# Edge stage of a graph layer: new pacing of its groups, and all output products of the attention ahead of the score table

## The chip, the core and the metric

The kernel runs on one core of a Trainium2 chip, in one launch. The metric is the device time in microseconds (us). Before the change three runs gave 2243.9 (median), 2245.11 and 2240.32.

Five engines have queues of their own and are ordered among each other by semaphores only: PE (TensorE, matrix products), DVE (VectorE), ACT (ScalarE), POOL (GpSimd, which here issues the gathers and scatters) and SP (SyncE, which here issues the loads of weights). All the code around the change is scheduled by hand: each engine executes its instructions in the order in which the program writes them.

## The reference

A graph of 625 nodes of 1024 features and 10000 edges goes through two layers. Layer 0 adds three things to the node matrix `x`, and layer 1 (which the change touches only in its first pieces) five more:

```
xn = layernorm(x)
# graph attention (GATv2): xl, xr = two projections of rms-normed, down-projected xn
e[edge]  = sum over 64 features of att * leaky(xl[src] + xr[dst])      # 4 heads
alpha    = softmax of e over the edges that end in the same node
graph    = segment_sum(alpha * xl[src]) @ W_up
# linear attention: q, k = elu(..)+1, v; 16 heads
mix      = ((q @ (k^T v)) / (q . sum k)) @ W_o + b_o
x        = x + graph + mix
x        = x + ternary_ffn(layernorm(x))          # weights rounded to -1, 0, 1
# layer 1: SAGE graph layers, linear attention again, attention and experts
```

The kernel turns the softmax into dense products: exp(e) of each edge is scattered into a table of 625 x 625 x 4 numbers in HBM, the table is read back tile by tile and multiplied with a matrix CT of edge counts.

## The kernel before

Nodes lie in five tiles of 125 (`t` = 0 to 4), features in eight blocks of 128 (`k`).

**The stream.** `do(prep, pe, after, after2)` writes a piece for PE; its `after` (work for DVE and ACT on the result) is written at the next call of `do`, its `after2` at the one after. So one piece of PE always stands between a product and its evaluation.

**The edge stage** (from about 48 us) lays two things over each other. On PE run the pieces of the linear attention: `key(t)` and `value(t)` for two halves of the features, each with up to six `count()` products (which build CT) behind it, then `states`, `query(m)`/`answer(m)` for m = 0 to 7, then `mixed(t)`, the output product of tile t with W_o (16 matmuls of 512 columns for each of two halves). Under them run 40 groups of edges: 39 of two chunks of 128 edges and one of 16 edges, 79 chunks in all. A chunk needs two gathers (`ga`, `gb`: rows of xl and xr, line L588) and one scatter (into `table`, L602) on POOL; a group needs three passes of DVE (L596, L568, L569) and a short limit (L571), and an exp on ACT (L575). `ga` and `gb` have four buffers each.

A **beat** writes a step of that second row: in beat g, exp of group g-3, scores of group g-2, gathers of group g, scatters of group g-3. Each piece of PE calls `work(us)` with the time that it is put at, and a beat is due whenever the sum passes a multiple of 7.6:

```
def work(us):                                            # before, L640 on
    beat["us"] += us
    while beat["us"] >= 7.6 * beat["g"] and beat["g"] < len(groups) + 3:
```

A gather of group g waits until the scores of group g-4 have left its buffers. A scatter waits until the scatter before it has landed, since both write `table`.

**The joint.** Before the table is read, PE has the first six k blocks of `mixed(0)`; what remains of the groups is written out; then come `load_table(0)` (POOL, tile `tb`), the sums of |weights| (L738), the rest of `mixed(0)`, the rounding of the weights (`ternary`, L753 to L756), `mixed(1)`, and `weigh(0)` (L774, five DVE multiplications that make `pT` from `tb` and CT).

**The steps p = 0 to 6** take one tile each, three stages deep: in step p, `sums(p)` (product `pg`), `weigh(p+1)`, `turn_sums(p)`, `up_again(p)` (product with W_up, which adds into the PSUM tile `px` that `mixed(p)` left open); the ternary FFN of tile p-1 (`ffn`: p1, f1, f2, f3, f4); normalisation and transposition of tile p-2 for layer 1 (p5, f5). Two places in each step are filled on PE by `spacer(p, c)`: the halves of `mixed(p+2)` while p is at most 2, `key` and `value` pieces of layer 1 afterwards. What is left of those pieces follows after step 6 with nothing between them.

Bias adds to `x` are at L1023, `up_again`'s add at L840, the first statistics of a step at L857.

Of the kernel before, what the change touches and what calls it, by code (L numbers as in the profile page):

```python
# [20 lines left out]
NT = 5  # L21
P = 125
# [31 lines left out]
def attempt(ctx: ExitStack, tc: tile.TileContext, w: dict, out: bass.AP, shifted: bool):  # L54
# [161 lines left out]
    class LinearAttention:  # L216
# [12 lines left out]

        def half(self, c):  # L230
            Wk, bk, Wv, bv = (w[n] for n in self.names[1:])
            self.wk, self.wv = Half(wpool, Wk, c), Half(wpool, Wv, c)
            self.bk, self.bv = self.bias(bk, c, "bk_t"), self.bias(bv, c, "bv_t")
            self.kf = mid([P, NT, 512], "kf")
            self.v = mid([P, NT, 4, 129], "v")
            nc.gpsimd.memset(self.v[:, :, :, 128:129], 1.0)
            self.kv.append(mix.tile([128, 4, 256], FP, tag="kv", name="kv", bufs=2))

        def key(self, t):
            kf, bk, wk = self.kf, self.bk, self.wk  # L240

            def pe():
                hold["pk", t] = ps1("pk")
                group(hold["pk", t][:P], [(self.xnT[:, k, nodes(t)], wk(k)) for k in range(KC)])

            def after():
                kb = mix.tile([P, 512], FP, tag="kb", name="kb", bufs=1)
                nc.vector.tensor_tensor(kb, hold.pop(("pk", t))[:P], bk[:P], op=ALU.add)
                ke = mix.tile([P, 512], FP, tag="ke", name="ke", bufs=1)
                nc.scalar.activation(ke, kb, AF.Exp)  # L250
                nc.scalar.activation(kb, kb, AF.Relu)
                hold["k", t] = ke, kb

            def after2():
                ke, kb = hold.pop(("k", t))
                nc.vector.scalar_tensor_tensor(kf[:, t, :], ke, 1.0, kb, op0=ALU.min, op1=ALU.add)

            do(None, pe, after, after2)
            self.work(6.9)

        def value(self, t):
# [11 lines left out]
            do(None, pe, after)  # L273
            self.work(6.9)

        def states(self):
# [5 lines left out]
            def state(a):  # L282
# [14 lines left out]
                do(None, pe, after, after2 if a == 3 else None)  # L297
                self.work(3.0)

            return [lambda a=a: state(a) for a in range(4)]  # L300

        def query(self, m):
# [16 lines left out]
            do(None, pe, after)  # L319
            self.work(8.5)  # L320

        def answer(self, m, oT):
# [13 lines left out]
            do(None, pe, after)  # L336
            self.work(3.5)

    with ExitStack() as st0:
# [8 lines left out]
        with ExitStack() as edges:  # L348
# [232 lines left out]

            def gather(g, j):
                lo, n, p = groups[g]
                if j == 0:
                    ab[g] = [pool.tile([128, G, 256], FP, tag=k, name=k, bufs=4) for k in ("ga", "gb")]
                if j < n:
                    for dst, src, ix in ((ab[g][0], xl_d, si), (ab[g][1], xr_d, di)):
                        nc.gpsimd.indirect_dma_start(  # L588
                            out=dst[0:p, j, :], out_offset=None, in_=src[:, :],
                            in_offset=bass.IndirectOffsetOnAxis(ap=ix[0:p, lo + j:lo + j + 1], axis=0))  # L590

# [6 lines left out]

            def scatter(g, j):
                lo, n, p = groups[g]  # L600
                if j < n:
                    nc.gpsimd.indirect_dma_start(  # L602
# [36 lines left out]

            beat = dict(us=0.0, g=0)  # L640

            def work(us):
                beat["us"] += us
                while beat["us"] >= 7.6 * beat["g"] and beat["g"] < len(groups) + 3:
                    g = beat["g"]
                    beat["g"] += 1
                    if 1 <= g <= NT:
                        self_loops(g - 1)
                    if g >= 3:
                        lo, n, p = groups[g - 3]  # L650
                        exp(es[0:p, lo:lo + n, :])
                    if 2 <= g < len(groups) + 2:
                        score_group(g - 2)
                    for j in range(G):
                        if g < len(groups):
                            gather(g, j)
                        if g >= 3:
                            scatter(g - 3, j)

            work(0.0)  # L660
            states = []
            for c in range(2):
                if c:
                    lin.half(c)
                for t in range(NT):
                    for f in (lin.key, lin.value):
                        f(t)
                        part["held"] = max(part["held"] - 1, 0)
                        for _ in range(6):
                            if count():  # L670
                                work(0.7)
                states.append(lin.states())
# [17 lines left out]

            def mixed(t, ks=range(KC)):
                for c in range(2):
                    def pe(c=c):
                        if c == 0 and ks[0] == 0:
                            hold["px", t] = ps2("px1")
                        for k in ks:
                            nc.tensor.matmul(hold["px", t][:P, c, :], lhsT=oT[:, k, nodes(t)], rhs=wo[c](k),  # L697
                                             start=(k == 0), stop=False)

                    yield lambda pe=pe: do(None, pe)  # L700

            for m in range(KC):
                if m + 1 < KC:
                    lin.query(m + 1)
                else:
                    for f in mixed(0, range(6)):
                        f()
                lin.answer(m, oT)
# [8 lines left out]
            nc.sync.dma_start(out=wu, in_=w["W_up"].rearrange("(k p) n -> p k n", p=128))  # L717
            bo = [lin.bias(w["L0_bo"], c, tag) for c, tag in enumerate(("bk_t", "bv_t"))]
            do.flush()
            while beat["g"] < len(groups) + 3:  # L720
                work(8.0)
            if not shifted:
# [4 lines left out]
        late = st0.enter_context(tc.tile_pool(name="l0r", bufs=1, reuse_waits="tile"))  # L727

        gu = wpool.tile([128, KC, 512], BF, tag="w", name="gu", padded_shape=[128, KC, 512])
        dn = late.tile([128, 2, D], BF, name="dn")  # L730
        made = [gu[:, :, 0:256], gu[:, :, 256:512], dn]
        part3 = late.tile([128, 3], FP, name="part3")
        wmean = late.tile([128, 3], FP, name="wmean")
        wscale = late.tile([128, 3], FP, name="wscale")

        def weight_sums():
            for i in range(3):
                nc.vector.tensor_reduce(part3[:, i:i + 1], raw[i], AX.X, ALU.add, apply_absolute_value=True)  # L738

        def weight_means():  # L740
            def pe():
                hold["pm"] = ps1("pm")
                group(hold["pm"][:, 0:3], [(ones, part3)])

            def after():
                nc.vector.tensor_scalar(wmean, hold["pm"][:, 0:3], 1.0 / (256 * D), 1e-5, op0=ALU.mult, op1=ALU.max)
                nc.vector.reciprocal(wscale, wmean)

            do(None, pe, after)

        def ternary(i):
            v = raw[i]
            nc.vector.tensor_scalar(v, v, wscale[:, i:i + 1], 1.0, op0=ALU.mult, op1=ALU.min)  # L753
            nc.vector.tensor_scalar(v, v, -1.0, MAGIC, op0=ALU.max, op1=ALU.add)
            m = made[i]
            nc.vector.tensor_scalar(m, v.rearrange("p (k n) -> p k n", k=m.shape[1]), MAGIC, None,  # L756
                                    op0=ALU.subtract)

# [70 lines left out]
        def up_again(t):  # L829
            px = hold.pop(("px", t))  # L830

            def pe():
                goT = hold.pop(("goT", t))
                for c in range(2):
                    for k in range(2):
                        nc.tensor.matmul(px[:P, c, :], lhsT=goT[:, k, :],
                                         rhs=wu[:, k, c * 512:(c + 1) * 512], start=False, stop=(k == 1))

# [123 lines left out]

        load_table(0)
        weight_sums()
        for f in mixed(0, range(6, KC)):
            f()
        weight_means()
        do()
        for i in range(3):
            ternary(i)  # L970
        for t in range(NT):
            rows_dma(nc.gpsimd, x[:, t, :], xrows[t])
            if t == 0:
                load_table(1)
        first_mixed = list(mixed(1))
        first_mixed[0]()
        weigh(0)
        first_mixed[1]()
        kv_pieces = iter([(f, t) for t in range(NT) for f in ("key", "value")])
        made_of = {}  # L980

        def spacer(p, c):

            if p + 2 < NT:
                if c == 0:
                    made_of["mixed"] = list(mixed(p + 2))
                made_of["mixed"][c]()
            else:
                f, t = next(kv_pieces)
                getattr(lin1, f)(t)  # L990

        for p in range(NT + 2):
            do()
            if p == NT - 2:
                lin1.half(0)
            if p >= 2:
                made_of[p - 2][5]()
            if 1 <= p <= NT:
                made_of[p - 1] = ffn(p - 1)
                made_of[p - 1][0]()  # L1000
            spacer(p, 0)
            if p >= 2:
# [15 lines left out]
            if p + 2 < NT:  # L1018
                load_table(p + 2)
            for t in range(2 * p, min(2 * p + 2, NT)):  # L1020
                for c in range(2):
                    xc = x[:, t, c * 512:(c + 1) * 512]
                    nc.vector.tensor_tensor(xc, xc, bo[c][:P], op=ALU.add)  # L1023
            if p <= NT:
                spacer(p, 1)
            if p < NT:
# [871 lines left out]
```

## Time and profile before

| | us |
|---|---|
| median of three runs | 2243.9 |
| the profiled execution | 2243.64 |
| its span, first to last instruction | 2241.8 |
| PE busy | 2126.3 (95%) |
| DVE busy | 713.6 (32%) |
| POOL busy | 347.6 (16%) |
| edge stage, first to last gather or scatter on POOL | 59.8 to 411.7 |
| first product of step 0 (`pg`) | 438.6 |
| first statistics of steps 1, 2, 3 (L857) | 455.7, 485.0, 513.9 |

The span is PE's nearly throughout, so a time is read as "what does PE wait for here, and at what clock does it run". Lines of a group give engine, operation, tiles, count, busy time, mean duration in ns, and the idle time ahead of it with what ended it. The profile shows a granted TensorE clock for each stretch (1.00 is full).

### The profile page before, as it was taken

To read this page: it belongs to the slowest core of one execution; us is meant where nothing else is said; L and a number is where in the kernel's file an instruction comes from. 1 tells how busy PE (TensorE), PEld (TensorE's weight loads), DVE (VectorE), ACT (ScalarE), POOL (GpSimd) and SP (SyncE) were. 2 spreads that over 40 slices of the span, in tenths; PEclk is the share of its full clock that TensorE was granted. 3 is DMA by queue.
4 is the path that set the end of the run, shared out by engine and by line. 5 is a ranking of instruction groups with operands and counts; after the bars stand their busy time and mean duration, and the time that the engine had idled before them with its cause. 6 is when DMAs were issued, how large, how long until landed. Compare 5 with 4: busy or idle time off the path is not lost. (4 is left out here: it accounts for less than half of the span.)

```text
span 2241.8 us, 17353 instructions
## 1 busy us (share of the span) xinstructions
PE 2126.3 (95%) x6934; PEld 1217.0 (54%) x6934; DVE 713.6 (32%) x1212; ACT 194.7 (9%) x354; POOL 347.6 (16%) x351
## 2 busy tenths in 40 slices
PE   7988788898899989999999999999999999999998
PEld 6655365454444657764445767556754444444443
DVE  4864556766421580000113124322111111111112
ACT  2100011011110210000000111110000000000000
POOL 1676767300000040010000000110000000000010
PEclk9999899998899999999999999999999999999999
DMA  9334253421122110231212111030198997898742
GB/s 286 114 108 136 67 175 102 113 83 47 38 85 75 41 54 1 75 141 38 75 38 103 38 38 38 19 103 29 65 334 320 332 330 279 325 332 296 267 148 93
DMA packets 145849, 301.63 MB, mean 135 GB/s; under 512 B 12370, under 2 KB 22436, under 8 KB 145754
## 3 DMA queue, kind: packets, MB, share of 16 engines
q1 hardware_dynamic: 123412, 243.18, 30.5%
q0 software_dynamic: 17664, 47.47, 7.1%
q10 hardware_dynamic: 4678, 9.72, 1.4%
q8 instruction: 58, 0.95, 0.2%
q14 instruction: 37, 0.30, 0.0%
HBM read 277.49 MB, written 22.84 MB: 134 GB/s over the span
## 5 line engine op out<-in xcount | busy, mean ns | idle before, releaser
L130 PE MATMUL pu<-w,xgT 128*128 128x512 f32 x768 | 333.9, 593 | 1.9 <-DVE xgT L1192 1.9
L130 PEld LDWEIGHTS pu<-w,xgT 128*128 128x128 f32 x768 | 144.0, 190 | 174.8 <-issue 172.0
L130 PE MATMUL pyb<-w,hb 128*128 128x512 f32 x384 | 174.3, 598 | 2.4 <-ACT yb L105 2.1
L130 PE MATMUL pq<-xnT,w 128*128 128x313 f32 x512 | 144.1, 441 | 16.1 <-DVE v L269 14.6
L130 PE MATMUL pk<-w,xnT 128*125 128x512 f32 x320 | 141.0, 593 | 4.7 <-DVE x L940 4.7
L130 PE MATMUL pv<-w,xnT 128*125 128x512 f32 x320 | 140.7, 592 | 1.2 <-ACT xnT L956 1.2
L130 PE MATMUL p<-tT,w 128*128 128x313 f32 x512 | 136.3, 428 | 0.4 <-DVE tT L1192 0.4
L130 PEld LDWEIGHTS pq<-xnT,w 128*128 128x128 f32 x512 | 100.3, 197 | 59.3 <-DVE v L269 15.4
L130 PEld LDWEIGHTS pyb<-w,hb 128*128 128x128 f32 x384 | 69.8, 189 | 90.9 <-issue 74.8
L130 PEld LDWEIGHTS p<-tT,w 128*128 128x128 f32 x512 | 96.8, 190 | 37.9 <-issue 1.2
L1732 DVE TENSOR_TENSOR su<-pu,su 128x512 f32<-128x512 f32 x24 | 16.6, 692 | 314.6 <-ACT su L1731 314.6
L130 PEld LDWEIGHTS pk<-w,xnT 128*125 128x125 f32 x320 | 59.4, 188 | 78.1 <-issue 71.2
L130 PEld LDWEIGHTS pv<-w,xnT 128*125 128x125 f32 x320 | 59.7, 188 | 73.3 <-issue 71.6
L1715 POOL DMA_INDIRECT xg<-rows_d,slots x12 | 11.4, 949 | 524.7 <-PE pxg L1722 448.9
L602 POOL DMA_INDIRECT table<-es,at x79 | 82.7, 1047 | 56.6 <-issue 25.5
L588 POOL DMA_INDIRECT ga<-xl_d,si x79 | 81.7, 1034 | 32.5 <-issue 21.7
L588 POOL DMA_INDIRECT gb<-xr_d,di x79 | 82.3, 1042 | 24.1 <-issue 23.8
L697 PE MATMUL px<-w,oT 128*125 128x512 f32 x160 | 75.0, 625 | 6.3 <-DVE oT L334 4.6
L130 PE MATMUL px<-w,hT 128*125 128x512 f32 x160 | 70.3, 592 | 0.0
L130 PE MATMUL px<-w,oT 128*125 128x512 f32 x160 | 70.3, 592 | 0.0
L130 PE MATMUL ph<-meanT,w 128*128 128x313 f32 x256 | 70.1, 426 | 0.0
L130 PE MATMUL ph<-xnT,w 128*128 128x313 f32 x256 | 70.0, 427 | 0.0
(365 smaller groups left out, 2476.5 us busy)
## 6 DMA issues: line engine op xcount, KB each, us to landing
w<-in_eW_dram SPq DMA_DIRECT2D x144, 1024.0 KB
w<-in_L_Wk_dram SPq DMA_DIRECT2D x8, 1024.0 KB
w<-in_L_Wv_dram SPq DMA_DIRECT2D x8, 1024.0 KB
w<-in_L_Wq_dram SPq DMA_DIRECT2D x8, 1024.0 KB
w<-in_L_Wo_dram SPq DMA_DIRECT2D x8, 1024.0 KB
w<-in_W_self_dram SPq DMA_DIRECT2D x8, 1024.0 KB
w<-in_W_neigh_dram SPq DMA_DIRECT2D x8, 1024.0 KB
w<-in_sW_dram SPq DMA_DIRECT2D x8, 1024.0 KB
```

What stands on the lines that cost most here:

```text
L130: nc.tensor.matmul(dst, lhsT=lhsT, rhs=rhs, start=(i == 0), stop=(i == len(pairs) - 1))
L588: nc.gpsimd.indirect_dma_start(out=dst[0:p, j, :], out_offset=None, in_=src[:, :], in_offset=bass.IndirectOffsetOnAxis(ap=ix[0:p, lo + j:l ...
L602: nc.gpsimd.indirect_dma_start(out=table[:, :], out_offset=bass.IndirectOffsetOnAxis(ap=at[0:p, lo + j:lo + j + 1], axis=0), in_=es[0:p, l ...
L697: nc.tensor.matmul(hold["px", t][:P, c, :], lhsT=oT[:, k, nodes(t)], rhs=wo[c](k), start=(k == 0), stop=False)
L1715: nc.gpsimd.indirect_dma_start(out=xg, out_offset=None, in_=rows_d[:, :], in_offset=bass.IndirectOffsetOnAxis(ap=slots[:, b:b + 1], axis=0))
L1732: nc.vector.tensor_tensor(su, pu[:, 0, :], su, op=ALU.mult)
```

## The change

- `work`: a beat is due every 8.2 instead of 7.6; pieces are put at other values: key and value 4.8 (6.9), a state 0.6 (3.0), a query 8.6 (8.5), an answer 2.7 (3.5), a count 0.72 (0.7); `mixed` now counts too, 0.6 for each k block of a half.
- Lags: scores 3 beats behind the gathers (2), exp 4 (3), scatters 5 (3). Ahead of the last output products the lags become 1, 1 and 2, and a beat then writes up to four scatters, each between two gathers, until they are caught up.
- All of `mixed(0)` to `mixed(4)` stand ahead of `load_table(0)`. Tiles 3 and 4 go first; their results, with the bias, are copied to SBUF (`kept`), which takes one of the four `mid` buffers until step 1. Tiles 0 to 2 stay open in PSUM.
- The sums of weights and `ternary` stand among these products. `x` is read (ten DMAs) between `load_table(0)` and `load_table(1)`.
- Steps 0 and 1 have no filler, step 2 one `key` piece in its second place, steps 3 to 5 two pieces, step 6 one: eight pieces instead of seven. The weights of layer 1's first half are asked for in step 0 (before: step 3), the tiles and biases of that half are made in step 1 (before: step 3).

```
-            self.work(6.9)
+            self.work(4.8)
...
-                while beat["us"] >= 7.6 * beat["g"] and beat["g"] < len(groups) + 3:
...
+            lags = [3, 4, 5]
...
+            def one_beat():
+                g = beat["g"]
+                beat["g"] += 1
+                if 1 <= g <= NT:
+                    self_loops(g - 1)
+                if lags[1] > lags[0]:
+                    raise_all(g - lags[1])
+                    scores(g - lags[0])
+                else:
+                    scores(g - lags[0])
+                    raise_all(g - lags[1])
+                for j in range(G):
+                    if g < len(groups):
+                        gather(g, j, 0)
+                        if lags[1] == lags[0]:
+                            scatter(g - lags[2])
+                        gather(g, j, 1)
+                    scatter(g - lags[2])
 
             def work(us):
                 beat["us"] += us
+                while beat["us"] >= 8.2 * beat["g"] and chunks:
+                    one_beat()
...
+            lags[:] = 1, 1, 2
+            kept = mid([P, 2, 2, 512], "kept")
+            mixed(3, keep=kept[:, 0])
+            weight_sums()
+            mixed(4, keep=kept[:, 1])
+            weight_means()
+            mixed(0, range(6, KC))
+            for t in (1, 2):
+                mixed(t)
+                ternary(t)
+            ternary(0)
             do.flush()
-            while beat["g"] < len(groups) + 3:
-                work(8.0)
+            while chunks:
+                one_beat()
...
         def up_again(t):
-            px = hold.pop(("px", t))
+            kept_apart = t >= 3
+            px = ps2("px1") if kept_apart else hold.pop(("px", t))
...
+                if p >= 3:
+                    spacer()
...
+            for t in ((0, 1), (2, 3, 4))[p] if p < 2 else ():
                 for c in range(2):
                     xc = x[:, t, c * 512:(c + 1) * 512]
-                    nc.vector.tensor_tensor(xc, xc, bo[c][:P], op=ALU.add)
+                    nc.vector.tensor_tensor(xc, xc, bo[c][:P] if t < 3 else kept[:, t - 3, c, :], op=ALU.add)
+            if p == 0:
+                lin1.weights(0)
+            if p == 1:
+                lin1.half(0, loaded=True)
+            if 2 <= p <= NT:
+                spacer()
```

(`scatter(last)` writes the oldest unwritten chunk if its group is at most `last`; `scores(last)` and `raise_all(last)` write scores and exps up to that group.)

## The prediction

> **What bounds the kernel now.** PE is busy 95% of the span, so I asked where the rest is. The table by stages comes first: columns are the stretch, its length, busy time of PE, PEld, DVE, ACT and POOL with instruction counts, then TensorE clock, DMA share and GB/s.
>
> ```profile
> 48.10:157.90 109.80, 109.76 (x469) 70.39 (x467) 81.73 (x212) 12.21 (x33) 74.05 (x74) 1.00 0.42 131
> 157.90:263.20 105.30, 90.38 (x287) 49.59 (x287) 54.80 (x120) 8.32 (x25) 77.04 (x75) 0.92 0.35 104
> 263.20:438.60 175.40, 139.48 (x444) 86.43 (x444) 112.29 (x123) 16.81 (x38) 112.15 (x113) 0.87 0.43 127
> ...
> 455.70:485.00 29.30, 27.89 (x108) 15.27 (x109) 19.28 (x37) 5.00 (x6) 1.41 (x2) 1.00 0.12 33
> 485.00:513.90 28.90, 26.32 (x111) 14.98 (x110) 20.75 (x42) 5.08 (x8) 1.71 (x4) 1.00 0.53 174
> 513.90:552.20 38.30, 33.34 (x114) 20.66 (x113) 21.58 (x44) 6.22 (x10) 0.00 (x0) 0.82 0.00 0
> ```
>
> Up to 158 PE has no gap. From there to 438.6 it is idle 14.9 + 35.9 = 51 us, at a mean clock of 0.92 and 0.87. The waits of that time (who waited for whom: total us, times, longest) say why:
>
> ```profile
> DVE ga L596 <- DMA gb<-xr_d,di: 105.6, 27, 8.4
> ...
> PE pq L130 <- DVE v L269: 14.6, 1, 14.6
> ...
> PE po L130 <- DVE oT L334: 10.4, 4, 3.7
> ...
> PE pkv L130 <- DVE v L269: 8.8, 1, 8.8
> ```
>
> PE waits for DVE, and DVE waits for gathers, which POOL issues. The page's groups give POOL's own pace:
>
> ```profile
> L602 POOL DMA_INDIRECT table<-es,at x79 | 82.7, 1047 | 56.6 <-issue 25.5
> L588 POOL DMA_INDIRECT ga<-xl_d,si x79 | 81.7, 1034 | 32.5 <-issue 21.7
> L588 POOL DMA_INDIRECT gb<-xr_d,di x79 | 82.3, 1042 | 24.1 <-issue 23.8
> ```
>
> With 0.30 us of issue between them (timeline of POOL) a chunk costs 1.03 + 1.04 + 1.05 + 0.9 = 4.02 us, 79 chunks 318 us, a beat of two 8.0 us. POOL starts at 59.8 and asks for the table at 413.4: 354 us, so it has only some 36 us of waits in the whole stage. **The edge stage is POOL's**; PE's stalls are its shadow. The timeline of PE at the joint shows the other half:
>
> ```profile
> 416.21 22.54 PE L697 MATMUL px<-w,oT 128*125 128x512 f32 x48
> 438.59 4.48 PE L130 MATMUL pg<-xl,pT 125*125 125x65 f32 x40
> 442.91 7.08 PE L697 MATMUL px<-w,oT 128*125 128x512 f32 x16
> ```
>
> Output products cover the reading of the table, and go on inside the steps.
>
> **What the Trainium skill says.** "TensorE: Matmul & The Clock Gate", Part 1: PE falls to half clock after about 3.4 us idle and needs about as long busy to return. The trace agrees in size: four `pd` matmuls take 1.22 us normally and 2.46 after the gap at 315; after the gap at 158 half clock lasted 5 us of work. "DMA: Bandwidth & Descriptors", Anatomy of one DMA: about 2.0 us fixed for a GpSimd DMA. The scatter's median to landing is 2.1 here. The same page, Latency and other measured facts: HBM latency rises to 2 us at high load. Here it rises more:
>
> ```profile
> table<-es,at POOLq DMA_INDIRECT x25, 2.1
> ...
> table<-es,at POOLq DMA_INDIRECT x4, 5.5
> ```
>
> The first is 190 to 290 with no weight load, the second 290 to 315 under 5.2 MB of loads.
>
> **Part 1: pacing.** PE's own work from 48.1 to the end of `mixed` is 20 x 6.87 (key, value) + 79 x 0.67 (counts) + 8.9 (states) + 8 x 8.43 (queries) + 8 x 2.11 (answers) + 5 x 13.7 (mixed) = 352 us. With lag 3 DVE should hardly wait for gathers, so PE should run nearly without gaps to **400**. All of the 51 us of idle and most of the half clock go.
>
> But the beats also pace POOL. Gather g needs the buffers of group g-4, whose scores are now written in beat g-1 (before: g-2), so POOL cannot start beat g before DVE has done beat g-1. A key or value with six counts puts in 4.8 + 6 x 0.72 = 9.12 and takes 10.87 us: one beat per 9.8 us. Without counts it is 6.87 x 8.2 / 4.8 = 11.7. Both exceed POOL's 8.0. The sums: 91.2 in the first half, 2.4 states, 61.7 in the second half; query(0) then puts the sum over 8.2 x 19, and beat 20 (164) falls into the first state. DVE writes it behind query(0)'s evaluation: PE reaches query(0) at about 243.8, ends it at 252.2, ACT 1.6, DVE 0.8, scores 2.3 = **256.9**. By then POOL has 42 chunks gathered and 32 scattered. Before, at 246 already, it had 45 and 39.
>
> From there POOL is behind and works without a pause (queries and answers: 11.3 of sum in 10.54 us, a beat per 7.7): 37 chunks x 2.68 of gathers = 99.2, 47 scatters x 1.35 = 63.4, so 419.5. Waits of scatters behind loads of weights are in the trace before at 299.9, 306.1, 311.8, 338.3, 355.3 and 393.4: 12.7 us together over the normal 0.3; the loads stay, so 432.2. The last scatters without gathers between them come 2.6 apart instead of 1.3 (393.4 to 413.4), four times: +5. New: 4 MB of layer 1's weights now load as soon as PE leaves W_o's tiles, at 390 to 405, under the scatters; 5.2 MB cost 7.2 us before, so +5 (bounds 0 and 10). **Table asked for at E = 442** (bounds 430 and 450) instead of 413.4. PE stands still from 400 on.
>
> **Part 2: the joint.** Sums of weights (6.7 us) and `ternary` (11.3) move to DVE's time under POOL: cost nothing, cover is DVE's idle time to 442. Saved: `weigh(0)` no longer stands behind them (428.1, with its table landed at about 422). Now: table lands 8.4 after E (before: 8.3), `weigh(0)` 4.9, so `pg` at E + 13.3. The x reads (ten DMAs on POOL, about 11 us) stand ahead of `load_table(1)`, which lands near E + 20, when `weigh(1)` wants it: cost 0, bounds 0 and 2. `kept`: four adds of 0.7 more, replaced one for one in step 1 but for bias adds; nothing. Two bias loads and a memset on POOL come in step 1, ahead of `load_table(4)`, whose table isn't wanted before step 3: nothing.
>
> **Part 3: steps 0 to 2 without fillers.** Before they took 17.1 (438.6 to 455.7), 29.3 and 28.9. PE work taken out is 13.7 in each, but DVE was busy 19.3 and 20.8 of the latter two, much of the rest being its chain through PE and ACT, so little comes back. From E: `pg` 6.4 (4.48 at full, 8.66 at half clock), `go` 1, `weigh(1)` 4.9, four bias adds 2.6, add of `up_again` 1.2 and small: step 1 begins at E + 30, 16.7 after `pg`. Step 1: to `room` 6.7, transposes 2.9, `pgu` 2 to 3.6, table load and tanh 2, DVE 2.2, `weigh(2)` 4.9, six adds 4.2 (before: four), hT and add 1.6, `pdn` and its evaluation 2.5: 28.5 (27 to 29.5). Step 2: 8.3 of statistics, `pg` at half clock to 12.4, then the same chain with a `key` evaluation (2.7, with ACT in it) instead of adds: 30 (28 to 34). So step 3 begins at E + 88.5 = **530.5** (before 513.9): +16.6. Steps 3 to 5 have two pieces as before, swapped: 0, bounds -4 and +3. The piece moved into step 2 leaves the gapless run after step 6: -6.9.
>
> Sum: +16.6 - 6.9 = **+9.7**. Everything later is PE's and only shifts. Against the profiled 2243.64 (span + 1.8) that is 2253.3; the median of the runs is 0.3 higher than that execution, so I say **2253**. A measurement of this kernel tells about 0.2%, 4.5 us, from no change.
>
> **Rivals.** *Faster: the stalls were the cost.* If POOL is not held back (beats written early enough, loads hidden in lag 5), E is 425; with steps of 27 each, step 3 begins at E + 83 = 508: -6 - 6.9 = -13, so 2231. For it: 51 us of idle that surely end. Against it: 36 us of waits are all that POOL had to give. It decides from E below about 428. *Slower by more: cold PE and contended scatters.* Weight loads cost 10, four scatters in a beat land later than 2.6 apart (+5), steps total 97: E = 452, step 3 at 549, +28: 2272. For it: clock 0.82 in step 3 before, where gaps were smaller than they will be. *It doesn't free PE:* `kept`'s adds stand on DVE behind scores that wait for gathers, and `mixed(1)` needs that PSUM. I expect at most 2 us of it; it costs nothing as PE has 50 us to spare before E + 13.
>
> **Numbers.** My forecast (E 434 to 450) 0.62, of which 0.11 within 0.2% and 0.02 faster; the faster rival 0.18 (0.14 faster, 0.04 within); the slower one 0.20 (0.02 of it within, for steps that turn out short). Faster 0.16, within 0.17, slower 0.67. Range: low 2237 is E at 430 with steps of 85 together (515; +1.1 - 6.9, less 1 for steps 3 to 5); high 2270 is just inside the slower rival. The forecast's own range is 2245 to 2262.
>
> **What would show it.** Right: no gap of PE over 2 us from 48 to about 400, clock 1.00 there; POOL waiting for DVE before 257 and for nothing but landings after; `tb` issued near 442; PE idle about 50 us ahead of `pg`; clock near 0.5 to 0.7 in steps 0 and 1; step 3 near E + 88. Wrong: `tb` before 428, or steps 0 to 2 in less than 70 us, makes it faster; PE still stalling in the queries means that DVE, not POOL's gathers, held it.

## The result, and the profile after

The changed kernel is slower: 2253.84 us (median of 12 runs, 2245.1 to 2256.75) beside 2241.05 (12 runs of the kernel before), ratio 1.0048, 95% interval 1.0038 to 1.0058. The profiled execution took 2254.41, its span is 2252.7: 10.9 more than the span of before.

The same table by stages as before the change (stretch, length, busy time of PE, PEld, DVE, ACT and POOL with counts, clock, DMA share, GB/s), cut where the changed kernel's own stages lie:

```profile
48.10:157.90 109.80, 109.80 (x468) 70.32 (x467) 78.15 (x213) 11.68 (x30) 64.41 (x66) 1.00 0.42 130
157.90:263.20 105.30, 104.52 (x388) 61.27 (x387) 51.13 (x106) 11.18 (x30) 60.25 (x61) 1.00 0.32 104
263.20:402.10 138.90, 138.88 (x428) 80.19 (x426) 98.72 (x107) 13.19 (x31) 95.19 (x93) 1.00 0.39 128
402.10:455.60 53.50, 0.00 (x1) 0.01 (x1) 19.24 (x31) 1.04 (x5) 34.29 (x35) 0.52 0.35 98
455.60:479.60 24.00, 20.82 (x90) 15.94 (x90) 12.93 (x17) 1.66 (x2) 4.63 (x8) 0.64 0.77 183
479.60:505.90 26.30, 13.88 (x34) 6.74 (x32) 20.43 (x39) 3.60 (x5) 2.66 (x5) 0.70 0.26 68
505.90:542.70 36.80, 29.37 (x98) 19.40 (x99) 20.97 (x43) 6.12 (x10) 2.00 (x3) 0.71 0.13 34
542.70:576.70 34.00, 27.76 (x114) 15.41 (x113) 21.42 (x44) 6.33 (x10) 0.00 (x0) 1.00 0.00 0
```

The first three lines are what the new pace did for PE: its busy time is the length, at clock 1.00, up to 402. The fourth is what it came to: PE then has nothing to do for 53.5 us. POOL's busy time in the second line is 60.25, where the kernel before had 77.04 in the same 105.3 us. So POOL did 16.8 us less of its work there.

The two waits that belong together, in the timeline of PE (start, length, tiles, and in brackets the idle time ahead with what ended it):

```profile
455.60 0.68 PE L130 MATMUL pg<-xl,pT 125*125 125x65 f32 x2 [53.52 <-DVE pT L818]
```

and in the timeline of POOL:

```profile
246.31 0.96 POOL L592 DMA_INDIRECT ga<-xl_d,si  x1 [6.21 <-DVE es L575]
...
257.39 1.47 POOL L592 DMA_INDIRECT ga<-xl_d,si  x1 [3.79 <-DVE es L575]
...
443.54 0.85 POOL L610 DMA_INDIRECT table<-es,at  x1 [1.91 <-issue]
446.05 0.90 POOL L164 DMA_DIRECT2D tb<-table  x1 [1.66 <-issue]
```

PE's wait ends with the multiplications of the table's first tile, and that tile is asked for at 446.05, directly behind the last scatter. This is 32.6 us later than in the kernel before, whose timeline of POOL has

```profile
413.43 0.90 POOL L164 DMA_DIRECT2D tb<-table  x1 [1.76 <-DMA table<-es,at]
```

POOL's waits up to then say why (who waited for whom: total us, times, longest; L573 and L575 are the last two operations of a group's scores). After:

```profile
POOL ga L592 <- DVE es L575: 22.2, 4, 7.2
...
POOL ga L592 <- DVE es L573: 8.9, 2, 5.2
```

Before, up to its own request at 413:

```profile
POOL ga L588 <- DVE ga L596: 0.6, 2, 0.3
```

Gathers waited 31.1 us for DVE to give back their buffers, and 0.6 before. That is nearly the whole of the 32.6; POOL's other waits nearly cancel, with 11.6 us more of its own issue time and 8.7 us less of waiting for landings.

### The profile page after: what moved, and what is told of

The parts are those of the page before. It is cut to its first block, busy times and chain, and to the rows that moved or that the text cites. A ratio compares the mean times of both kernels' runs of the same rounds, so it can differ in the third digit from the quotient of the medians.

```text
span 2252.7 us, 17353 instructions
## 1 busy us (share of the span) xinstructions
PE 2117.4 (94%) x6934; PEld 1212.6 (54%) x6934; DVE 715.3 (32%) x1216; ACT 194.7 (9%) x354; POOL 342.6 (15%) x351
## 5 line engine op out<-in xcount | busy, mean ns | idle before, releaser
L130 PE MATMUL pq<-xnT,w 128*128 128x313 f32 x512 | 138.1, 428 | 2.0 <-ACT qf L319 1.2
L1748 POOL DMA_INDIRECT xg<-rows_d,slots x12 | 11.3, 943 | 524.8 <-PE pxg L1755 449.0
L130 PE MATMUL pg<-xl,pT 125*125 125x65 f32 x200 | 32.4, 332 | 57.4 <-DVE pT L818 55.1
L592 POOL DMA_INDIRECT gb<-xr_d,di x79 | 81.1, 1026 | 25.8 <-issue 25.8
L130 PE MATMUL px<-w,oT 128*125 128x512 f32 x160 | 70.3, 592 | 0.0
```

What stands on the lines that cost most here:

```text
L130: nc.tensor.matmul(dst, lhsT=lhsT, rhs=rhs, start=(i == 0), stop=(i == len(pairs) - 1))
L592: nc.gpsimd.indirect_dma_start(out=ab[g][side][0:p, j, :], out_offset=None, in_=src[:, :], in_offset=bass.IndirectOffsetOnAxis(ap=ix[0:p, ...
L1748: nc.gpsimd.indirect_dma_start(out=xg, out_offset=None, in_=rows_d[:, :], in_offset=bass.IndirectOffsetOnAxis(ap=slots[:, b:b + 1], axis=0))
```

## The experiments

The twelve experiments ran in three sets of four. In the first two sets (e1 to e8) the kernel before itself took 2285 us (single runs from 2272 to 2303), and in the third (e9 to e12) 2243 (2239 to 2246); so a ratio belongs to its own set. In the first two sets the engines stood still for waits that the profile doesn't explain (told under e6 and e9), and what decides about the cause is the third.

### Set 1: the pace undone, alone, and at measured values; the order of pieces

**e1_old_pace**: the changed kernel with the work values of before.

```
-            self.work(4.8)
+            self.work(6.9)
...
-                while beat["us"] >= 8.2 * beat["g"] and chunks:
+                while beat["us"] >= 7.6 * beat["g"] and chunks:
```

> The changed kernel with the old values of the pieces (6.9, 3.0, 8.5, 3.5, 0.7) and a beat each 7.6, lags and order as changed. Pacing theory (POOL was held back early, so the table came late): POOL runs without waiting for DVE from about 85 us, the table is asked for near 405 to 415 instead of 446, some PE stalls return in the edge stage (up to 30 us, as a beat falls due every 7.0 us and POOL needs 8.0), the output products then cover the reading of the table; time 2222 to 2236. Rival (the loss is that of fillers missing in steps 0 to 2, wherever the table lies): 2248 or more.

Measured: 2308.94 us, ratio 1.0087 (1.0054 to 1.012). The expectation was wrong. The table was asked for at 494, 27 us behind the last scatter, and this wait was for the last of `ternary` on DVE, which stands behind the products. Moving all products ahead of the table makes the table wait for PE and DVE too, when they are late. Nor did POOL run freely, as the expectation had it: its gathers waited 57.2 us for DVE, more than the changed kernel's 31.1. The unexplained waits (see e6) lie in this time, so this run doesn't tell what the old pace does without them.

**e2_pace_alone**: the kernel before with the new work values, lags and the catching up of lags; products and steps as before.

```
-            self.work(6.9)
+            self.work(4.8)
...
-                while beat["us"] >= 7.6 * beat["g"] and beat["g"] < len(groups) + 3:
+                while beat["us"] >= 8.2 * beat["g"] and chunks:
...
+            lags[:] = 1, 1, 2
```

> The kernel before with the new pacing and lags alone; all output products, sums of weights, reads and fillers where they were. Pacing theory: table asked for near 441, PE idle for most of 345 to 446, first product of step 0 near 467 instead of 438.6, steps as before: 2262 to 2276. Rival (the pacing is harmless or a gain, the order is the loss): 2236 to 2246.

Measured: 2296.38, ratio 1.0034 (1.0012 to 1.0056): slower as expected, by about a third of the size. The table was asked for at 471.8, and steps 1 to 5 took what they took before.

**e3_true_pace**: the changed kernel with the times that the trace shows for each piece (a key's 16 matmuls 6.87 us, a query's 32 8.43), and a beat of 8.0, POOL's own price of two chunks.

```
-            self.work(4.8)
+            self.work(6.87)
...
-                while beat["us"] >= 8.2 * beat["g"] and chunks:
+                while beat["us"] >= 8.0 * beat["g"] and chunks:
```

> The changed kernel with each piece put at what PE takes in the trace (key and value 6.87, state 1.1, query 8.43, answer 2.11, count 0.67, a k block of an output product 0.86) and a beat each 8.0, POOL's own pace. Pacing theory: POOL hardly waits for DVE, PE hardly for anything; table asked for near 407 with PE done near 402; steps as in the changed kernel: 2214, from 2208 to 2224, faster than both. Rival (POOL is slower for another reason, loads of weights under its scatters): table still after 430, 2240 or more.

Measured: 2287.06, ratio 1.0009 (0.999 to 1.0027); table at 476.0. Far from the 1.2% expected, and the numbers of the rival.

**e4_value_first**: the kernel before with `value` ahead of `key` in the steps' fillers.

```
-        kv_pieces = iter([(f, t) for t in range(NT) for f in ("key", "value")])
+        kv_pieces = iter([(f, t) for t in range(NT) for f in ("value", "key")])
```

> The kernel before with one edit: the pieces of layer 1 in the order value, key instead of key, value, so that the first filler of steps 3 to 5 is a value. Theory: the key's evaluation (DVE add, two ACT passes, DVE) in front of the transposes opens the gaps of 1.9 and 1 us that put PE at half clock in steps 3 to 5 (0.82, 0.86, 0.93); with a value there the clock stays near 1.00 and the three steps shorten by about 9 us together: 2232 to 2235. Rival (the steps were shorter in the changed kernel for their shifted phase): within 3 us of the kernel before.

Measured: 2280.18, ratio 0.9975 (0.9956 to 0.9994), so about 5.7 us faster. The trace agrees where the edit lies. Steps 3, 4 and 5 of this kernel, by stages:

```profile
558.40:594.60 36.20, 30.74 (x113) 18.22 (x112) 21.48 (x43) 6.33 (x10) 0.00 (x0) 0.91 0.00 0
594.60:629.20 34.60, 29.50 (x113) 15.99 (x112) 16.73 (x38) 6.33 (x10) 0.00 (x0) 0.95 0.05 12
629.20:654.10 24.90, 20.24 (x63) 9.83 (x62) 14.79 (x34) 6.07 (x9) 0.00 (x0) 0.96 0.19 68
```

They sum to 95.7; in the kernel before they took 38.2, 37.4 and 25.8 (by the first statistics of each step), 101.4 in sum. That is 5.7 us less, of the 9 expected. The same work at clocks of 0.91 to 0.96 where the kernel before had 0.82, 0.86 and 0.93.

### Set 2: the same questions again, and the lag

**e5_lag_two**: the changed kernel with all lags one beat shorter until the last products.

```
-            lags = [3, 4, 5]
+            lags = [2, 3, 4]
```

> The changed kernel with lags of 2, 3, 4 in place of 3, 4, 5 while the pieces run (lags[:] = 1, 1, 2 at the end stays). Theory (the slower pace of the beats together with lag 3 and four gather buffers holds POOL back: gather g needs the scores of group g-4, which DVE writes in beat g-1; with lag 2 in beat g-2): POOL passes 257 us with one beat, two chunks, more behind it, so the table is asked for some 8 us earlier, near 438 instead of 446, and the time against the kernel before goes from 1.0048 to about 1.001 (0.999 to 1.003). PE may stall for DVE again in the queries as before, which costs nothing while it ends its pieces before 430. Rival (POOL is bound by its own 318 us and by landings of scatters under weight loads, wherever it stands at 257): table at 446 as before, ratio 1.004 to 1.006. Second rival (DVE now waits for gathers and puts off the pieces): products end later than the scatters, ratio above 1.006.

Measured: 2283.9, ratio 0.9994 (0.9971 to 1.0018), table at 468.4. POOL's gathers waited 15.7 us for DVE, but 28.2 us of waits of scatters for exps on ACT came in. The ratio lies in the range expected; the table's time does not. Without the changed kernel's own ratio in this set it decides nothing.

**e6_true_pace_again** is e3's kernel.

> The same kernel as e3_true_pace: work values as the timeline of PE measures them (key and value 6.87, state 1.1, query 8.43, answer 2.11, count 0.67, product 0.86 per block) and beats of 8.0, the rest as changed. In e3 PE's instructions came up to 2.1 us apart for stretches with nothing to wait for, 32 us in sum, which neither of the first two profiles has. Without them: beats come at POOL's own 8.0, POOL is not held back, table asked for near 420 (415 to 430), PE ends its pieces by 425, step 1 starts 33.6 after the table; ratio to before 0.994 (0.990 to 0.998). Rival (e3's stalls were not the cause, the early beats make DVE wait and PE with it, so that the last product and ternary end behind the scatters): table at 440 or later, ratio 1.000 to 1.005.

Measured: 2285.1, ratio 1.0002 (0.9983 to 1.0022), table at 463.8: the rival's numbers. But PE stood still again, 27 us in sum, with nothing that it waited for. In its timeline:

```profile
136.52 1.01 PE L130 MATMUL pv<-w,xnT 128*125 128x512 f32 x1 [1.51 <-issue]
138.64 1.01 PE L130 MATMUL pv<-w,xnT 128*125 128x512 f32 x1 [1.11 <-issue]
140.06 1.01 PE L130 MATMUL pv<-w,xnT 128*125 128x512 f32 x1 [0.41 <-issue]
```

Single matmuls start up to 2.1 us apart ("issue"). In the profile of the kernel before there is none of this. DVE stood still as well: of the three lines below, from the timelines of PE, DVE and POOL, the first is the product of a `key`, done at 211.3. Its add on DVE starts 18.5 us later, and the profile names no instruction of this core that it waited for ("remote"). The gather in the third line needs a buffer of the scores behind this add and waits 8.5 us.

```profile
204.31 7.03 PE L130 MATMUL pk<-w,xnT 128*125 128x512 f32 x16
229.82 0.69 DVE L252 TENSOR_TENSOR kb<-pk,bk_t 125x512 f32<-125x512 f32 x1 [21.80 <-remote]
234.88 1.47 POOL L592 DMA_INDIRECT ga<-xl_d,si  x1 [8.46 <-DVE es L575]
```

So POOL's waits in this kernel look like those of the changed one:

```profile
POOL ga L592 <- DVE es L575: 40.2, 6, 14.0
...
POOL ga L592 <- DVE es L573: 10.4, 2, 9.5
```

They needn't come from the pace, though: what gives the buffers back is DVE, and DVE stood still too, with its product ready as far as the trace shows. This run supports neither the theory nor its rival.

**e7_old_pace_again** is e1's kernel.

> The same kernel as e1_old_pace: the new order of the products with the old work values and beats of 7.6. e1 had the table's first load wait 27 us for ternary on DVE, behind the products, and had 35 us of PE's unexplained gaps. Theory (the order needs PE done with its pieces when the last scatter is issued; with the old pace PE stalls for DVE's waits on gathers as before, some 50 us, and ends the five products near 450, ternary behind them): table asked for at 450 to 465 whatever POOL does, ratio 1.004 to 1.012. Rival (only the pace is at fault, the order alone gains): table near 415 to 425, ratio 0.990 to 0.996.

Measured: 2305.42 us, ratio 1.0071 (1.0049 to 1.0093). The ratio is the theory's, the way to it isn't: the table was asked for at 488.75 instead of 450 to 465, and PE's waits for DVE that the theory names are not in the trace, where PE had 78 us of the unexplained gaps instead. Whether its own waits would have done it isn't shown. The wait at the joint, in POOL's timeline:

```profile
457.01 0.85 POOL L610 DMA_INDIRECT table<-es,at  x1 [1.91 <-DMA table<-es,at]
488.75 0.92 POOL L164 DMA_DIRECT2D tb<-table  x1 [30.88 <-DVE gu L761]
```

The scatters were done at 457; the table was read 31 us later.

**e8_pace_alone_again** is e2's kernel.

> The same kernel as e2_pace_alone: the new pace and lags on the order before, where the rest of the products cover the reading of the table and go on inside the steps. e2's joint was that of before (steps 1 to 5 took 29.3, 28.9, 38.4, 37.4 and 25.8). Theory: the table is asked for about 30 us later (446 instead of 413), PE waits for it with its pieces of the edge stage done, and nothing is won back: +20 to +30 us, ratio 1.009 to 1.013. Rival (the table comes later only by what the moved weight loads cost, and pacing alone is neutral): ratio 0.998 to 1.004.

Measured: 2293.97, ratio 1.0043 (1.0029 to 1.0058), table at 461.4. What the theory names is in the trace: PE stood still for the end of the edge stage with its pieces done,

```profile
460.45 0.59 PE L130 MATMUL pm<-part,ones 128*128 128x3 f32 x2 [74.01 <-DVE part L761]
```

but the ratio is below what the theory expects, and just above the rival's. The kernel before, in this set, had lost time in its edge stage too (see e9); how much of the 74 us stands against that isn't shown.

### Set 3: both kernels traced, the reads, and the two together

**e9_before_traced**: the kernel before.

> The kernel before itself, for a trace on the chip of the experiments, where its median is 2285 and not 2241. Theory (PE's instructions come up to 2.1 us apart for stretches of the edge stage with no wait shown, as in e1 to e8, and that is the whole difference): idle of PE put down to issue is 35 to 50 us between 48 and the first pg, none after, the table is asked for at 445 to 455 instead of 413.4, and steps 1 to 5 take 29.3, 28.9, 38.2, 37.4 and 25.8 as on the first chip. Rival (gathers and scatters are slower on this chip): no such gaps, a chunk on POOL takes over 4.3 us instead of 4.0.

Measured: 2242.41 us, span 2240.6, no gap of PE put down to issue, table at 412.4, steps 29.3, 28.9, 38.2, 37.4 and 25.8. Here the kernel runs as in its first profile, so this run cannot tell what made it slower in the first two sets. Where it was slower can be told: e4's kernel is this one up to the steps, and its step 1 starts at 500.1 where this one's starts at 454.7, so the 42 us between the sets lie ahead of the steps. Between 48 and 410 us the waits that name nothing ("issue" and "remote") sum to 10 to 75 us on PE, 20 to 107 on DVE and 36 to 91 on ACT in the traces of the first two sets, and to at most 2.6 on each of them in the six other traces. Sets 2 and 3 ran on the same chip, so it isn't a chip that is slower throughout. Where these waits come from stays open.

**e10_after_traced**: the changed kernel.

> The changed kernel itself, for its ratio and its trace on the chip of the experiments. If gaps of PE's instructions of 20 to 45 us come here too, part of them fall into the 53 us in which PE waits for the table anyway, while the kernel before pays all of them: ratio to before 1.000 to 1.004 instead of 1.0048, table asked for at 455 to 470. If the gaps delay DVE, and with it POOL, in full, they are paid here too: ratio 1.0048 again or more. The joint is that of the first profile in either case: step 1 starts 33.6 after the table, steps 1 to 5 take 26.3, 36.7, 34.0, 32.9 and 24.5.

Measured: 2254.59, ratio 1.0058 (1.0036 to 1.0081). The unexplained waits didn't come, so both conditions of the expectation are empty, except for the joint: step 1 starts 32.5 us after the table is asked for (33.6 in the first profile), and steps 1 to 5 take 26.6, 37.2, 34.0, 32.9 and 24.4. The run repeats the result.

**e11_reads_behind**: the second table ahead of the reads of x in POOL's queue.

```
         load_table(0)
+        load_table(1)
         for t in range(NT):
             rows_dma(nc.gpsimd, x[:, t, :], xrows[t])
-        load_table(1)
```

> The changed kernel with load_table(1) ahead of the ten reads of x in POOL's queue. Theory (weigh(1) on DVE waited 3.9 us for the second table behind these reads, and the whole step 1 with it): second table lands 20 or less after the first is asked for instead of 25, step 1 starts 29.5 to 31 after it instead of 33.6, time 2 to 4 us under e10: ratio 0.001 to 0.0018 lower than that of e10. Rival (the x rows are then late for up_again's add, or pg at half clock ends behind weigh(1) anyway): step 1 at 33 or later, ratio as e10 within 0.0006.

Measured: 2250.98, ratio 1.0039 (1.0025 to 1.0053), 3.6 us below e10, with intervals that overlap. DVE no longer waits for the second table (in its timeline `go`, which ends the first product, is followed at once by `weigh(1)`),

```profile
459.89 0.42 DVE L855 TENSOR_TENSOR go<-pg,den 125x256 f32<-125x256 f32 x1
460.23 4.85 DVE L818 TENSOR_TENSOR pT<-tb,CT 125x500 f32<-125x500 f32 x5
```

and step 1 starts 31.2 after the first request (469.6 after 438.4), 1.3 to 2.4 less than in the changed kernel's two profiles: at the edge of what the theory said. A gain of some 2 us is in the trace; the rest of the 3.6 isn't explained by it. The profiled execution is the fastest of the eight (2246.22), and its table is asked for 8.3 us earlier than e10's, which the edit, written behind that request, doesn't explain either; POOL's first gather already starts 4.4 us earlier than in the changed kernel's first profile.

**e12_true_pace_reads**: e6's work values, its beat of 8.0 among them, and e11's order of reads; the lags stay 3, 4, 5.

> True work values (e6) and load_table(1) ahead of the x reads (e11) together. If both reasons hold, the two gains add, as they lie in different stages: table asked for at 455 to 465, step 1 29.5 to 31 after it, ratio to before 0.0015 under e6's 1.0002, so 0.9985 (0.9965 to 1.0005). If PE's last product or its clock holds step 1 (in e6 PE had no long gap before pg, so pg runs at full clock), the reads gain nothing more: ratio 1.000.

Measured: **2222.76 us, ratio 0.9916 (0.9896 to 0.9936)**: faster than both kernels, and 28.2 us below e11, from which it differs in the work values and the beat alone. The stages:

```profile
48.10:157.90 109.80, 109.80 (x487) 71.95 (x486) 84.41 (x221) 12.08 (x35) 70.59 (x70) 1.00 0.43 137
157.90:263.20 105.30, 104.52 (x372) 60.50 (x371) 54.69 (x109) 11.52 (x31) 77.12 (x76) 1.00 0.36 117
263.20:412.10 148.90, 131.42 (x395) 75.92 (x394) 105.67 (x116) 12.69 (x31) 97.58 (x96) 0.94 0.29 93
412.10:424.50 12.40, 9.62 (x23) 3.95 (x21) 1.07 (x2) 0.00 (x0) 6.12 (x10) 0.97 0.99 251
424.50:444.60 20.10, 17.55 (x69) 13.26 (x69) 12.85 (x18) 1.66 (x2) 4.30 (x8) 0.59 1.04 261
444.60:470.80 26.20, 15.72 (x56) 8.48 (x54) 20.40 (x39) 3.61 (x5) 2.67 (x5) 0.75 0.61 150
470.80:507.30 36.50, 29.07 (x97) 19.27 (x98) 20.91 (x42) 6.11 (x10) 1.99 (x3) 0.71 0.13 35
```

POOL's busy time in the second line is back at 77.12. At 257 us it has gathered 50 chunks, where e11 had 43. Its gathers' waits for scores, 30.0 us in e11, are one up to the table's request:

```profile
POOL ga L592 <- DVE es L573: 0.9, 1, 0.9
```

and the two ends meet, in POOL's timeline

```profile
412.10 0.89 POOL L164 DMA_DIRECT2D tb<-table  x1 [1.76 <-PE px L724]
```

and in PE's

```profile
387.69 0.58 PE L130 MATMUL pm<-part,ones 128*128 128x3 f32 x2 [13.54 <-DVE part L743]
388.13 33.58 PE L724 MATMUL px<-w,oT 128*125 128x512 f32 x72
424.52 0.68 PE L130 MATMUL pg<-xl,pT 125*125 125x65 f32 x2 [2.81 <-DVE pT L818]
```

The table is asked for at 412.1, 26.3 us earlier than in e11 and as early as in the kernel before (413.4), and PE ends its products at 421.7, 2.8 us ahead of the first `pg`. This is what the new order needs: both ends at the same time. The two profiled executions lie 27.2 us apart (2246.22 and 2218.98), and the 26.3 are nearly all of it. The expectation missed the size; it added to e6's ratio, from a set with the unexplained waits. Its other half, step 1 at 29.5 to 31 after the request, was missed too: step 1 starts 32.5 after it, as in e10. DVE didn't wait for the second table, but the first took 11.3 us to come (8.5 in the changed kernel), in a stretch whose DMA share is 0.99 with layer 1's weights loading. So the order of the reads isn't shown to help here.

## Why the prediction was right, and where its terms were not

The forecast was 2253 and the measurement 2253.84; by the profiled executions, +9.7 was forecast and +10.8 measured. That the kernel gets slower, and through POOL, was reasoned and came so; that the sum is met within some 1 us is luck, as two large errors cancel. The terms:

| term | predicted | measured |
|---|---|---|
| PE's idle time from 48 to 402 | none over 2 us | 0.8 in all |
| POOL starts beat 20; chunks gathered and scattered | 256.9; 42, 32 | 257.4; 42, 32 |
| table asked for | 442 | 446.05 |
| step 1 after that | 30 | 33.6 |
| step 1, step 2 | 28.5, 30 | 26.3, 36.7 |
| step 3 starts | 530.5 | 542.7 |
| steps 3 to 5 against before | 0 (-4 to +3) | -10.1 |
| the piece moved into step 2 (up to layer 1's first query) | -6.9 | -6.7 |

**The mechanism was right**, and e12 beside e11 shows it, since these two differ in the work values and the beat alone: the beats' pace, through buffers that DVE gives back late, sets when POOL ends, and nothing in PE's gained 51 us was worth anything while POOL ended 33 us later. The longer lag alone isn't the loss, as e12 has it too; whether the slow pace would cost as much with a lag of 2 isn't shown, as e5 ran with the unexplained waits. The *faster* rival (table at 425) was the wrong one for this pace and the right one for another: its condition, beats written early enough, is met in e12. The *slower* rival had cold PE in the steps and 97 us from the table's request to step 3; 96.6 came, where the forecast had 88.5. It had the request at 452, too late by 6, and no gain in steps 3 to 5. *It doesn't free PE* named a wait of DVE behind the scores that would stop PE: nothing of it in the changed kernel, but 13.5 us in e12, at the sums of weights, which there stand behind scores that wait for gathers (the line at 387.69).

**Three terms were mis-sized, and by luck they cancel.** Up to step 3 the forecast is 12.2 us short (4.1 at the table's request, 3.6 from there to step 1, -2.2 in step 1, 6.7 in step 2), and steps 3 to 5 give 10.1 back, which it had put at 0. Without these 10.1 the time would have been 2264.5, above the forecast's own range of 2245 to 2262.

1. *Table at 442, x reads at no cost*: 4.1 and 3.6 short. The 4.1 lie within its bounds and were not taken apart. The 3.6 begin in POOL's timeline:

```profile
450.27 0.52 POOL L165 DMA_DIRECT2D x<-in_x_dram  x1
454.35 0.55 POOL L164 DMA_DIRECT2D x<-in_x_dram  x1 [3.56 <-DMA tb<-table]
...
459.16 0.86 POOL L164 DMA_DIRECT2D tb<-table  x1 [1.32 <-issue]
```

POOL paused 3.6 us in the midst of the ten reads until the first table had landed. Even so they took 11.6 us of POOL (447.58 to 459.16), close to the 11 that the estimate gave them. What it had too small is the landing: the second table took up to 11.6 us from its issue, behind the reads, where the median of the tables is 8.4. DVE's timeline shows what that cost:

```profile
471.09 4.88 DVE L818 TENSOR_TENSOR pT<-tb,CT 125x500 f32<-125x500 f32 x5 [3.85 <-DMA tb<-table]
```

2. *Step 2 of 30*: 36.7, outside its bounds of 28 to 34. In part this is a sum: the terms that the prediction lists for this step add up to 33.2 and not to 30 (those of step 1 to 29.0 and not to 28.5). The rest is PE's part of the chain at a clock of 0.71: `pg` ends 14.0 us into the step and not 12.4, and `px` takes 5.18 us where step 2 of the kernel before had 3.7. Only the `key`'s evaluation was priced; its product, 7.03 us on PE, also stands ahead of `px`, and DVE waits for that:

```profile
539.89 1.23 DVE L886 TENSOR_TENSOR x<-px,x 125x1024 f32<-125x1024 f32 x1 [4.48 <-PE px L881]
```

3. *Steps 3 to 5: two pieces as before, swapped, 0*: -10.1, outside its bounds. This term compared amounts of work and not the order. Before, step 3 in the timeline of PE:

```profile
520.39 0.59 PE L955 MATMUL ptr<-ident,xn 125*128 125x125 f32 x4
522.92 0.87 PE L955 MATMUL ptr<-ident,xn 125*128 125x125 f32 x4 [1.94 <-DVE kb L248]
524.72 8.66 PE L130 MATMUL pg<-xl,pT 125*125 125x65 f32 x40 [0.93 <-ACT xnT L956]
```

After:

```profile
549.12 0.59 PE L1001 MATMUL ptr<-ident,xn 125*128 125x125 f32 x4
550.39 0.65 PE L1001 MATMUL ptr<-ident,xn 125*128 125x125 f32 x4 [0.68 <-ACT xnT L1002]
551.71 4.58 PE L130 MATMUL pg<-xl,pT 125*125 125x65 f32 x40 [0.68 <-ACT xnT L1002]
```

With a `key` at the head of the step, the transposes' second half waits 1.94 us for the key's evaluation on DVE, and `pg` behind it runs at half clock, 8.66 for 4.58. With a `value` the gap is 0.68 and the clock holds. e4 makes this swap alone and gains 5.7 of the 10.1. The rest was not taken apart; those steps ran at 0.91 to 0.96 in e4 and near 1.00 after, so it goes with the clock; why that is higher after isn't shown.

The sum by stages against the kernel before: table +32.6, from there to step 1 -8.7, step 1 -3.0, step 2 +7.8, steps 3 to 5 -10.1, later pieces -6.7, small -1.0. Without the first term the change gains some 22 us, and e12, whose table comes as early as before, gained 20.6.

One reading of the prediction goes too far: it set the scatter's time to landing, 2.1 and 5.5 us, beside the figure for the latency of HBM that it cites. The lines show that landings took 3.4 us longer under the loads of weights; how much of that is latency and how much waiting in queues they don't show.

**Not tried:** the old pace, the pace alone, the lag of 2 and the true pace alone where there are no unexplained waits; each of the moved weight loads; a fifth gather buffer.

## What to carry to other kernels

Where the instructions of one engine are paced by the written times of another's, count at a fixed moment how far the paced queue has come (here 42 gathered chunks at 257 us, where the kernel before had 48 and e12 50), and look for waits on buffers that come free a beat later than they did. Taking stalls from an engine that isn't the bound only moves its wait to the end; what counts is that the two chains end together. And the order of two equal pieces of filler matters when the evaluation of one stands in front of the next product.

## What the runs showed of the hardware

- Half clock did not need a long wait of PE. In e12 PE paused 2.8 us ahead of `pg`, in the changed kernel 53.5, and yet the next three stretches have similarly low clocks: 0.59, 0.75, 0.71 in e12 and 0.64, 0.70, 0.71 after (455.6 to 479.6, steps 1, 2). Step 3 of the kernel before fell to half clock (`pg` 8.66 us for 4.58) with no gap over 1.94 us. The Trainium skill, "TensorE: Matmul & The Clock Gate", Part 1, speaks of about 3.4 us idle; its section "A second HAM failure mode: psum-queue depth-cycling" says of another kernel, which cycles through banks of PSUM, that short idle times between groups of matmuls make the clock swing between half and full. These traces, with idle times of 0.27 to 2.81 us around the slow products, fit that section better, though here the idle times are waits for DVE and ACT.
- POOL issued eight DMAs and then waited until the oldest had landed, in the changed kernel (two of the table, six of x, then 3.6 us), in e11 (four and four, then 3.6 us) and in e12 (four and four, then 6.2 us): whoever puts DMAs with long landings in a row counts that wait with them. Whether the chip sets the eight or the program's semaphores do isn't shown.
- PE stood still between matmuls of the edge stage, with nothing awaited, in all eight traces of the first two sets (10 to 78 us in sum), DVE and ACT stood still in the same traces, and none of it came in the other six executions that were traced. The kernel before took 42 us longer in those sets. The cause is open.
